# Block transposes of an attention layer: split by head, moved in longer pieces, and one pair of tiles in eight given to TensorE

## Chip, cores and metric

The kernel runs on one core of one Trainium2 chip. The metric is the device time of one execution in microseconds (us). Three runs of the kernel before took 2395.11, 2396.89 and 2406.44 us; the median is 2396.89.

## What is computed

The input x is 4 batches of 1024 tokens by 256 channels, with a context of 77 tokens per batch. Four blocks follow one another: L0 (self attention, cross attention and a feed-forward), L1 (three attention layers of 4 heads), L2 and L3 (cross attention of 16 heads). The change concerns the second and third layers of L1, in which a sequence attends to itself. Cut to one such layer:

```python
def _mha_layer(q, k, v, Wq, bq, Wk, bk, Wv, bv, gamma, beta):   # q = k = v = enc, (4, 1024, 256)
    Q = jax.nn.relu(q @ Wq + bq); K = jax.nn.relu(k @ Wk + bk); V = jax.nn.relu(v @ Wv + bv)
    ...                                                          # 4 heads of 64 channels
    scores = jnp.einsum('hbqd,hbkd->hbqk', Qh, Kh) / jnp.sqrt(jnp.float32(dh))
    scores = jnp.where(key_mask[None, :, None, :] == 0.0, NEG, scores)
    attn = jax.nn.softmax(scores, axis=-1)
    attn = attn * query_mask[None, :, :, None]
    out = jnp.einsum('hbqk,hbkd->hbqd', attn, Vh)
    ...
    return _layer_norm(out + q, gamma, beta)

enc = _mha_layer(...); enc = jax.nn.leaky_relu(enc @ Wff[i] + bff[i], negative_slope=0.2) + enc
```

All of it is float32. The weights of a query (its row of exp(scores)) must be transposed before the product with V, because TensorE contracts over partitions: scores come out with queries on partitions and keys along the row, and the product needs keys on partitions.

## The kernel before

**Items and units.** Work is cut into items: one layer for one batch. The class `Self4` (L1121) is an item of an L1 self layer; there are eight (two layers, four batches), one after the other. An item has 16 units: two pairs of heads p = 0, 1, and for each eight query tiles t of 128 rows (`attend`, L1247). `Pipe.unit` (L139) writes the instructions of one unit in a fixed order of stages: what is due under "full", then the scores of this unit, then what is due under "next", then `pump()`, then "turn", "late" and "col". `Pipe.later(kind, delay, f)` (L132) puts f under a stage of the unit that is `delay` units later. `pump()` adds, spread by given costs, the steps of other items: the end of the item before (statistics, norm L1583 and L1586, the transposes L1396, the feed-forward L1405 to L1412) and the start of the next one (transposes L1167, mask row L1179, values L1190, query and key projections L1226 and L1233).

**Order of instructions.** TensorE (PE) executes in the order in which the program was written. For VectorE (DVE), ScalarE (ACT), GpSimd (POOL) and the SyncE queue (SP) a scheduler decides the order when the program is built; each engine then executes its own list in order, waiting on semaphores.

**One unit.**
- `scores` (L1255): PE computes a 128 x 1024 tile of scores for each of the two heads of the pair, in four products (L1262; the profile shows each as two). They go to two PSUM tiles `ss` of the pool `pb`, which has two buffers; the loop is over key halves outside and heads inside, so the first head's two products are not adjacent.
- For each head, DVE takes the negative maximum along the row (L1273), and ACT takes exp with that bias, summing the row (L1279). The result goes to the tile `PR`, which holds two query tiles and two heads and has two buffers (tag "E"). The exp writes so that 32-wide key blocks of the same residue c of 4 lie together.
- `turned_by_blocks` (L1285), due at "next" of the following unit: DVE transposes every 32 x 32 block of the unit's two heads in place, in one instruction 2048 wide (L1291). After every second tile, 16 DMAs of 128 KB (L1298) move the blocks from 32 partitions of `PR` to 32 partitions of `PT` (two buffers, tag "B"), 8 issued by SP and 8 by POOL in turn. Each moves four pieces of 1 KB from each of 32 partitions.
- `weighted` (L1324), due at "turn" two and three units after that: PE multiplies by V in two halves, 16 matmuls each in the profile (L1334), into a PSUM tile `po`, which ACT copies out (`carry`, L1509, copy L1512).
- `normal` (L1346): PE transposes the result back (L1352), DVE scales it by the row sums (L1357 to L1362) and adds it to x (L1364).

The pool `p1` (L2090) has four PSUM tiles of 128 x 512; projections, transposes and `po` all take theirs from it.

The function `turned` (L1306) is the other way to transpose: 16 PE transposes of 128 x 128 per query tile, four to a PSUM tile, and a copy of each PSUM tile to `PT`. It stands in the kernel for other kinds of mask (`net.blocks` false, L1985 to L1987), and is not executed here. `evac` (L1495) gives copies in turn to DVE and ACT; `carry` gives them to ACT when `net.blocks` is true.

Of the kernel before, what the change touches and what calls it, by code (L numbers as in the profile page):

```python
# [13 lines left out]
ALU = mybir.AluOpType  # L14
AX = mybir.AxisListType
PSUM = bass.MemoryType.PSUM

P = 128
NB, S, C, SC = 4, 1024, 256, 77
NT = S // P  # L20
# [102 lines left out]
class Pipe:  # L123
# [15 lines left out]
    def unit(self, scores=None, cost=0.0):  # L139
        self.call("full")  # L140
        if scores:
            scores()
        self.call("next")
        self.now += cost
        self.pump()
        for kind in ("turn", "late", "col"):
            self.call(kind)
        self.u += 1

    def run(self, items):  # L150
        pump = Pump(self, 1, items[0].start(), [])
        pump.until(lambda: items[0].halves >= 1)
        left = pump.lists[0]
        before = None
        for a, b in zip(items, items[1:]):
            b.prev = a
        for i, item in enumerate(items):
            last = i + 1 == len(items)
            first = left + ([] if last else items[i + 1].start())
            second = (before.end() if before else []) + (item.end() if last else [])  # L160
            left = []
            idle = item.idle()
            self.pump = pump = Pump(self, item.units + idle, item.more() + first, second)
            for _ in range(idle):
                self.unit()
            for scores in item.attend():
                self.unit(scores, item.cost)
            assert last or not any(pump.lists)
            before = item
        while self.due:  # L170
            pump.n = 0
            self.unit()
        pump.n = pump.units - 1
        pump()
# [33 lines left out]
class Cross16(Item):  # L208
# [147 lines left out]
    def scores(self, g, c):  # L356

        net, h = self.net, H16
        nc = net.nc
        e, s = g // 2, g % 2  # L360
        if g % 2 == 0:
            self.pts = net.tile("B", [SC, 2, h.J, 512], name="PT")
        pt = self.pts[:, g % 2]
        pbs = [net.pb.tile([P, 2, 512], F32, tag="pb", name="pb") for _ in range(2)]
        for j in range(h.J):
            rows = slice(32 * j, 32 * j + 32)
            nc.tensor.matmul(  # L367
                pbs[j // 2][:SC, j % 2, :], self.ka[rows, e, 2 * (j % 2) + s, :], self.qt[rows, e, ts(c, 512)],
                start=True, stop=False,
            )  # L370
        for j in range(h.J):
            rows = slice(32 * j, 32 * j + 3 * G)
            nc.tensor.matmul(  # L373
                pbs[j // 2][:SC, j % 2, :], net.pick16[rows, g, :], self.sh[rows, c, :], start=False, stop=True
            )
        for i in range(2):
            nc.scalar.activation(pt[:, 2 * i : 2 * i + 2, :], pbs[i][:SC], AF.Exp, scale=self.l.scale)  # L377
        net.pipe.later("col", 0, lambda: self.weighted(g, c, pt))

    def weighted(self, g, c, pt):  # L380
        net, l, h = self.net, self.l, H16
        nc = net.nc
        po = net.p1.tile([P, 512], F32, tag="p1", name="po")
        for j in range(h.J):
            col = self.head(g, j) * h.vs
            nc.tensor.matmul(  # L386
                po[ts(j, h.slot), :], l.v[:, self.b, col : col + h.vw], pt[:, j, :], start=True, stop=True
            )
        ot = net.tile("OT", [P, 512], name="OT")
        net.evac(ot, po)  # L390
        net.pipe.later("late", 1, lambda: self.normal(g, c, ot))
# [249 lines left out]
class Layer16Self:  # L641


    scale, norm, eps, out, ff, has_wo = 0.25, 1, None, None, None, True
# [168 lines left out]
class LayerFew:  # L813
# [3 lines left out]
    scale, norm, eps, out, ff, has_wo = 0.25, 1, None, None, None, True  # L817
# [303 lines left out]
class Self4(Item):  # L1121
# [133 lines left out]
    def scores(self, p, t):  # L1255
        net = self.net
        nc = net.nc
        ss = [net.pb.tile([P, 2, 512], F32, tag="pb", name="ss") for _ in range(2)]
        for k in range(2):
            for h in range(2):  # L1260
                rows = slice(64 * h, 64 * h + 64)
                nc.tensor.matmul(  # L1262
                    ss[h][:, k, :], self.qk[p][rows, 0, ts(t, P)], self.qk[p][rows, 1, ts(k, 512)],
                    start=True, stop=True,
                )
        if not net.blocks:
            pr = net.tile("E", [P, 2, S], name="PR")
        elif t % 2 == 0:
            self.pr = net.tile("E", [P, 2, 2, S], name="PR")
        for h in range(2):  # L1270
            at = slice(2 * p + h, 2 * p + h + 1)
            s2 = ss[h].rearrange("p k n -> p (k n)")
            nc.vector.tensor_reduce(self.nm[:, t, at], s2, AX.X, ALU.max, negate=True)  # L1273
            if net.blocks:
                out = self.pr[:, t % 2, h, :].rearrange("p (c k i) -> p k c i", c=4, i=32)
                s2 = s2.rearrange("p (k c i) -> p k c i", c=4, i=32)
            else:
                out = pr[:, h, :]
            nc.scalar.activation(out, s2, AF.Exp, bias=self.nm[:, t, at], accum_out=self.sums[:, t, at])  # L1279
        if net.blocks:  # L1280
            net.pipe.later("next", 1, lambda pr=self.pr: self.turned_by_blocks(p, t, pr))
        else:
            net.pipe.later("full", 1, lambda: self.turned(p, t, pr))

    def turned_by_blocks(self, p, t, pr):  # L1285


        net = self.net
        nc = net.nc
        part = pr[:, t % 2].rearrange("p h s -> p (h s)")  # L1290
        nc.vector.transpose(part, part)  # L1291
        if t % 2 == 0:
            return

        pt = net.tile("B", [P, 2, 2, 4, NT, 32], name="PT")
        for c in range(4):
            for a in range(4):
                (nc.sync, nc.gpsimd)[a % 2].dma_start(  # L1298
                    out=pt[ts(c, 32), :, :, a].rearrange("p t h k j -> p (t h) (k j)"),
                    in_=pr[ts(a, 32), :, :, ts(c, 256)].rearrange("p t h n -> p (t h) n"),  # L1300
                )
        state = []
        for half in range(2):
            net.pipe.later("turn", 2 + half, lambda half=half: self.weighted(p, t, pt, half, state))

    def turned(self, p, t, pr):  # L1306

        net = self.net
        nc = net.nc
        if t % 2 == 0:  # L1310
            self.pt = net.tile("B", [P, 2, 2, NT, P], name="PT")
        pts = self.pt
        for h in range(2):
            for k in range(0, NT, 4):
                pm = net.p1.tile([P, 4, P], F32, tag="p1", name="pm")
                for i in range(4):
                    nc.tensor.transpose(pm[:, i, :], pr[:, h, ts(k + i, P)], net.ident)
                net.evac(pts[:, t % 2, h, k : k + 4, :], pm)
        if t % 2:
            state = []  # L1320
            for half in range(2):
                net.pipe.later("col", half, lambda half=half: self.weighted(p, t, pts, half, state))

    def weighted(self, p, t, pts, half, state):  # L1324
        net = self.net
        nc = net.nc
        if half == 0:
            state.append(net.p1.tile([P, 2, P], F32, tag="p1", name="po"))
        po = state[0]
        if net.blocks:  # L1330
            po = po.rearrange("p t (a j) -> p t a j", a=4)
        for k in range(4 * half, 4 * half + 4):
            for h in range(2):
                nc.tensor.matmul(  # L1334
                    po[64 * h : 64 * h + 64], self.v[:, k, 64 * (2 * p + h) : 64 * (2 * p + h) + 64],
                    pts[:, :, h, :, k, :] if net.blocks else pts[:, :, h, k, :], start=k == 0, stop=k == NT - 1,
                )
        if half:
            if t % 4 == 1:
                self.ot = net.tile("OT", [P, 4, P], name="OT")  # L1340
            at = t % 4 - 1
            net.carry(self.ot[:, at : at + 2, :], state[0])
            if at:
                net.pipe.later("late", 1, lambda ot=self.ot: self.normal(p, t - 3, ot))
# [853 lines left out]
```

## Time and profile before

| | |
|---|---|
| median of three runs | 2396.89 us |
| the profiled execution | 2396.79 us |
| its span, first to last instruction | 2394.9 us |
| mean granted TensorE clock | 0.958 |
| busy: PE, DVE, ACT, POOL | 2204.3, 1582.6, 930.2, 380.4 us |
| the eight items of the self layers, from 948.2 to 1872.7 us | 924.5 us |
| busy there: PE, DVE, ACT, POOL | 878.7, 771.2, 440.2, 295.1 us |
| block transposes (L1291) | 128 of 2311 ns |
| block DMAs (L1298) | 1024 of 128 KB |

The profile gives one execution. Busy time of an engine is the union of its instructions' spans; matmuls are pipelined, and a matmul that waits inside its span counts as busy. A group's row gives line, engine, operation, tiles written and read, count, then busy time and mean duration, then the idle time of the engine just before these instructions with what ended it. In a timeline a row is start, duration, engine, line, operation, with neighbours of one kind merged; in brackets stands idle time before it and what ended it. SPq marks the issuing of DMAs by SP.

### The profile page before, as it was taken

Reading aid. Unit: us, or ns where it says so; the run is one execution under the profiler, and the core shown is the slowest. Engines: PE = TensorE matmul, PEld = TensorE weight load, DVE = VectorE, ACT = ScalarE, POOL = GpSimd, SP = SyncE. Lnnn points to the kernel's source line nnn. Section 1 sums busy time; section 2 is a strip of 40 time slices with the busy share of each in tenths; the row PEclk is TensorE's granted clock in tenths of the full one; section 3 lists DMA queues with packets and bytes.
Section 4 is the critical chain, followed back from the end, with each engine's and each line's share of the span. In section 5 each row is a group of like instructions: output and inputs, shape, how many; then the busy total and the mean of one; then the engine's idle time right before and its main releaser. Section 6 shows DMA issues by size and latency. Waiting matters only on the chain. (4 is left out here: it accounts for less than half of the span.)

```text
span 2394.9 us, 31195 instructions
## 1 busy us (share of the span) xinstructions
PE 2204.3 (92%) x11035; PEld 1204.8 (50%) x11035; DVE 1582.6 (66%) x3167; ACT 930.2 (39%) x1828; POOL 380.4 (16%) x648
## 2 busy tenths in 40 slices
PE   6899999999898979999999899999999899999996
PEld 3565446566577655545454445454545344444442
DVE  6665553534424565888888788888888656656765
ACT  2222332222232355545454454444444234434333
POOL 2000000000000000333333233333333100000000
PEclk8999989989998998999999999999999899999988
DMA  5000010000000000667776577766787400000000
GB/s 147 1 3 14 5 36 1 1 3 5 12 1 7 1 5 1 146 147 152 151 156 144 123 151 157 151 142 141 148 163 143 97 5 1 5 1 1 27 18 28
DMA packets 148677, 158.01 MB, mean 66 GB/s; under 512 B 51432, under 2 KB 130849, under 8 KB 148513
## 3 DMA queue, kind: packets, MB, share of 16 engines
q1 hardware_dynamic: 122161, 85.63, 17.2%
q0 software_dynamic: 25296, 69.24, 13.1%
q8 instruction: 91, 1.49, 0.3%
q10 hardware_dynamic: 1056, 1.05, 0.1%
q14 instruction: 73, 0.60, 0.1%
HBM read 17.41 MB, written 4.19 MB: 9 GB/s over the span
## 5 line engine op out<-in xcount | busy, mean ns | idle before, releaser
L1279 ACT ACTIVATE PR<-ss,nm 128x1024 f32<-128x1024 f32 x256 | 284.7, 1114 | 366.2 <-DVE nm L1273 290.2
L1291 DVE STREAM_TRANSPOSE PR<-PR 128x2048 f32<-128x2048 f32 x128 | 295.8, 2311 | 128.9 <-ACT PR L1279 114.3
L1298 POOL DMA_DIRECT2D PT<-PR x512 | 279.6, 554 | 577.7 <-PE ss L1262 236.7
L1262 PE MATMUL ss<-QK 64*128 64x512 f32 x1024 | 324.8, 628 | 28.8 <-ACT PR L1279 28.5
L1273 DVE TENSOR_REDUCE nm<-ss 128x1 f32<-128x1024 f32 x256 | 299.6, 1210 | 13.8 <-PE ss L1262 13.8
L377 ACT ACTIVATE PT<-pb 77x1024 f32<-77x1024 f32 x192 | 185.4, 1015 | 193.2 <-PE pb L373 193.2
L1334 PE MATMUL po<-PT,V 128*64 128x256 f32 x2048 | 251.1, 387 | 5.1 <-DMA PT<-PR 5.1
L281 DVE TENSOR_REDUCE mx<-pa 128x4 f32<-128x308 f32 x384 | 161.4, 470 | 83.7 <-PE pa L276 82.5
L1262 PEld LDWEIGHTS ss<-QK 64*128 64x128 f32 x1024 | 113.3, 187 | 176.8 <-ACT PR L1279 99.7
L1334 PEld LDWEIGHTS po<-PT,V 128*64 128x64 f32 x2048 | 136.6, 137 | 108.4 <-issue 51.1
L276 PE MATMUL pa<-KA,QT 64*128 64x308 f32 x768 | 169.1, 486 | 14.0 <-DVE mx L281 12.8
L1545 POOL TENSOR_TENSOR pw<-va,minus_half 128x4 f32<-128x4 f32 (+1 forms) x28 | 38.8, 1384 | 714.5 <-DVE va L1543 542.0
L386 PE MATMUL po<-PT,Vc 77*32 77x512 f32 x768 | 140.4, 639 | 7.6 <-ACT PT L377 7.0
L276 PEld LDWEIGHTS pa<-KA,QT 64*128 64x128 f32 x768 | 84.3, 193 | 99.1 <-issue 37.0
L604 PE MATMUL pp<-hF,w 128*128 128x256 f32 x512 | 116.9, 382 | 0.0
L367 PE MATMUL pb<-QT,KA 32*77 32x512 f32 x768 | 114.1, 665 | 0.0
L619 PE MATMUL pp<-w,hid 128*128 128x256 f32 x512 | 113.7, 379 | 0.0
L619 PEld LDWEIGHTS pp<-w,hid 128*128 128x128 f32 x512 | 97.0, 190 | 16.5 <-issue 2.2
L604 PEld LDWEIGHTS pp<-hF,w 128*128 128x128 f32 x512 | 95.6, 190 | 18.2 <-issue 6.0
L266 PE MATMUL pp<-hT,wq 128*128 128x512 f32 x192 | 98.0, 646 | 5.5 <-ACT hT L1507 5.0
L1536 DVE BATCH_NORM_STATS2 st<-x 128x6 f32<-128x256 f32 x256 | 97.7, 403 | 3.2 <-DMA x<-in_x 2.3
L1405 PE MATMUL pp<-wo,hE 128*128 128x256 f32 x384 | 96.4, 393 | 1.6 <-ACT hE L1512 1.6
(256 smaller groups left out, 3079.5 us busy)
## 6 DMA issues: line engine op xcount, KB each, us to landing
PT<-PR SPq DMA_DIRECT2D x512, 128.0 KB
PT<-PR POOLq DMA_DIRECT2D x512, 128.0 KB, 4.9
x<-in_x SPq DMA_DIRECT2D x4, 1024.0 KB
out<-x SPq DMA_DIRECT2D x8, 512.0 KB
w<-in_ff_w SPq DMA_DIRECT2D x2, 1024.0 KB
gb<-in_norms POOLq DMA_DIRECT2D x5, 256.0 KB, 6.6
wk<-in_l_wk SPq DMA_DIRECT2D x10, 128.0 KB
wv<-in_l_wv SPq DMA_DIRECT2D x5, 256.0 KB
```

Of the source, the lines that this page charges most:

```text
L276: nc.tensor.matmul(pas[i], self.qt[rows, e, ts(t, P)], self.ka[rows, e, :, :], start=True, stop=True)
L281: nc.vector.tensor_reduce(out, pas[i].rearrange("p (j s) k -> p j s k", s=2), AX.X, ALU.max, negate=True)
L377: nc.scalar.activation(pt[:, 2 * i : 2 * i + 2, :], pbs[i][:SC], AF.Exp, scale=self.l.scale)
L386: nc.tensor.matmul(po[ts(j, h.slot), :], l.v[:, self.b, col : col + h.vw], pt[:, j, :], start=True, stop=True)
L604: nc.tensor.matmul(pp[:, i, :], self.w1[:, cc, ts(f + i, P)], s["hT"][:, cc, ts(q, 2 * P)], start=cc == 0, stop=cc == NC - 1)
L619: nc.tensor.matmul(pp[:, u, :], s["a"][:, f, ts(u, P)], self.w2[:, f, :], start=f == 0, stop=f == NF - 1)
L1262: nc.tensor.matmul(ss[h][:, k, :], self.qk[p][rows, 0, ts(t, P)], self.qk[p][rows, 1, ts(k, 512)], start=True, stop=True,)
L1273: nc.vector.tensor_reduce(self.nm[:, t, at], s2, AX.X, ALU.max, negate=True)
L1279: nc.scalar.activation(out, s2, AF.Exp, bias=self.nm[:, t, at], accum_out=self.sums[:, t, at])
L1291: nc.vector.transpose(part, part)
L1298: (nc.sync, nc.gpsimd)[a % 2].dma_start(out=pt[ts(c, 32), :, :, a].rearrange("p t h k j -> p (t h) (k j)"), in_=pr[ts(a, 32), :, :, ts(c, ...
L1334: nc.tensor.matmul(po[64 * h : 64 * h + 64], self.v[:, k, 64 * (2 * p + h) : 64 * (2 * p + h) + 64], pts[:, :, h, :, k, :] if net.blocks e ...
```

## The change

Three things, all in `scores`, `turned_by_blocks`, `turned` and `weighted`:

1. `PR` and `PT` are laid out anew. `PR` is now [4 key residues c, 2 tiles, 2 heads, 256] per partition, and `PT` is [4 source blocks a, 2 tiles, 2 heads, 8, 32]. Each of the 16 DMAs then moves one piece of 4 KB from each of 32 partitions. SP issues 12 of them (a = 0, 1, 2) and POOL 4 (a = 3).
2. The block transposes are one instruction per head, 1024 wide, and are written in `scores` right after the exps; `issue_after` keeps them behind the second reduction in DVE's list.
3. For p = 1 and tiles 2 and 3, the fourth of the item's eight DMA groups is replaced by `turned`: 32 PE transposes and 8 copies by ACT. Tile 2 is due at "next" two units later, tile 3 at "turn" one unit later, both in the unit of tile 4; the products with V are due in the units of tiles 6 and 7, where they were before.

```diff
+        blocks = net.blocks and (p, t // 2) != (1, 1)
         if not net.blocks:
             pr = net.tile("E", [P, 2, S], name="PR")
         elif t % 2 == 0:
-            self.pr = net.tile("E", [P, 2, 2, S], name="PR")
+            self.pr = net.tile("E", [P, 4, 2, 2, S // 4], name="PR")
+        if net.blocks and not blocks:
+            pr = self.pr.rearrange("p c t h n -> p (c t h n)")[:, ts(t % 2, 2 * S)].rearrange("p (h n) -> p h n", h=2)
...
-            nc.vector.tensor_reduce(self.nm[:, t, at], s2, AX.X, ALU.max, negate=True)
-            if net.blocks:
-                out = self.pr[:, t % 2, h, :].rearrange("p (c k i) -> p k c i", c=4, i=32)
+            reduced = nc.vector.tensor_reduce(self.nm[:, t, at], s2, AX.X, ALU.max, negate=True)
+            if blocks:
+                out = self.pr[:, :, t % 2, h, :].rearrange("p c (k i) -> p k c i", i=32)
...
-        if net.blocks:
-            net.pipe.later("next", 1, lambda pr=self.pr: self.turned_by_blocks(p, t, pr))
+        if net.blocks and not blocks:
+            net.pipe.later(("next", "turn")[t % 2], 2 - t % 2, lambda: self.turned(p, t, pr))
+        elif net.blocks:
+            with net.tc.issue_after(reduced.ins):
+                for h in range(2):
+                    part = self.pr[:, :, t % 2, h, :]
+                    nc.vector.transpose(part, part)
+            if t % 2:
+                net.pipe.later("next", 1, lambda pr=self.pr: self.turned_by_blocks(p, t, pr))
...
-        part = pr[:, t % 2].rearrange("p h s -> p (h s)")
-        nc.vector.transpose(part, part)
-        if t % 2 == 0:
-            return
-        pt = net.tile("B", [P, 2, 2, 4, NT, 32], name="PT")
+        pt = net.tile("B", [P, 4, 2, 2, NT, 32], name="PT")
         for c in range(4):
             for a in range(4):
-                (nc.sync, nc.gpsimd)[a % 2].dma_start(
-                    out=pt[ts(c, 32), :, :, a].rearrange("p t h k j -> p (t h) (k j)"),
-                    in_=pr[ts(a, 32), :, :, ts(c, 256)].rearrange("p t h n -> p (t h) n"),
+                (nc.gpsimd if a == 3 else nc.sync).dma_start(
+                    out=pt[ts(c, 32), a].rearrange("p t h k j -> p (t h k j)"),
+                    in_=pr[ts(a, 32), c].rearrange("p t h n -> p (t h n)"),
                 )
...
-                net.evac(pts[:, t % 2, h, k : k + 4, :], pm)
+                net.carry(pts[:, t % 2, h, k : k + 4, :], pm)
...
-                net.pipe.later("col", half, lambda half=half: self.weighted(p, t, pts, half, state))
+                when = ("turn", 2 + half) if net.blocks else ("col", half)
+                net.pipe.later(*when, lambda half=half: self.weighted(p, t, pts, half, state, False))
```

More of the change, by code (lines that the diff above doesn't have):

```diff
@@ L1321, in turned, with weighted @@
             for half in range(2):
-                net.pipe.later("col", half, lambda half=half: self.weighted(p, t, pts, half, state))
-    def weighted(self, p, t, pts, half, state):
+                when = ("turn", 2 + half) if net.blocks else ("col", half)
+                net.pipe.later(*when, lambda half=half: self.weighted(p, t, pts, half, state, False))
+    def weighted(self, p, t, pts, half, state, blocks=True):
         net = self.net
@@ L1329, in weighted @@
         po = state[0]
-        if net.blocks:
+        if blocks:
             po = po.rearrange("p t (a j) -> p t a j", a=4)
@@ L1335, in weighted @@
                     po[64 * h : 64 * h + 64], self.v[:, k, 64 * (2 * p + h) : 64 * (2 * p + h) + 64],
-                    pts[:, :, h, :, k, :] if net.blocks else pts[:, :, h, k, :], start=k == 0, stop=k == NT - 1,
+                    pts[:, :, :, h, k, :].rearrange("p a t j -> p t a j") if blocks else pts[:, :, h, k, :], start=k == 0, stop=k == NT - 1,
                 )
```

## Prediction

> **What bounds the kernel now.** I read the page first. In its forty slices the change can touch only the 17th to 32nd, where DMA is busy at 4 to 8 tenths: the two self layers of L1, eight items (two layers by four batches) of 16 units each. A unit is one query tile of one pair of heads. Then I asked for engine times in the eight windows from one item's first scores to the next one's; two of them, and the sum of the eight:
>
> ```profile
> 1413.40:1526.40 113.00, 108.32 (x545) 54.11 (x543) 96.28 (x123) 55.59 (x119) 37.57 (x67) 1.00 0.73 154
> 1643.60:1758.00 114.40, 109.70 (x546) 54.51 (x544) 96.42 (x122) 53.33 (x105) 37.01 (x66) 1.00 0.71 150
> sum 924.50, PE 878.73 PEld 433.56 DVE 771.23 ACT 440.16 POOL 295.10; mean PE 109.84 PEld 54.20 DVE 96.40 ACT 55.02 POOL 36.89
> ```
>
> After the length come the busy times of PE, PEld, DVE, ACT and POOL, the clock and the DMA share. PE is busy 878.7 of 924.5 us, idle 45.8; DVE 771.2. PE looks like the bound, but the groups and the timeline say how much of its busy time is waiting:
>
> ```profile
> L1262 PE MATMUL ss<-QK 64*128 64x512 f32 x1024 | 324.8, 628 | 28.8 <-ACT PR L1279 28.5
> L1291 DVE STREAM_TRANSPOSE PR<-PR 128x2048 f32<-128x2048 f32 x128 | 295.8, 2311 | 128.9 <-ACT PR L1279 114.3
> ```
> ```profile
> 1558.51 1.99 PE L1262 MATMUL ss<-QK 64*128 64x512 f32 x8
> ```
> ```profile
> 1314.50 1.95 PE L1334 MATMUL po<-PT,V 128*64 128x256 f32 x16
> 1314.81 2.31 DVE L1273 TENSOR_REDUCE nm<-ss 128x1 f32<-128x1024 f32 x2
> ...
> 1316.03 1.11 ACT L1279 ACTIVATE PR<-ss,nm 128x1024 f32<-128x1024 f32 x1 [2.91 <-DVE nm L1273]
> ...
> 1317.16 1.11 ACT L1279 ACTIVATE PR<-ss,nm 128x1024 f32<-128x1024 f32 x1
> ...
> 1317.28 3.11 PE L1262 MATMUL ss<-QK 64*128 64x512 f32 x8 [0.83 <-ACT PR L1279]
> ...
> 1318.39 2.31 DVE L1291 STREAM_TRANSPOSE PR<-PR 128x2048 f32<-128x2048 f32 x1 [1.27 <-ACT PR L1279]
> ...
> 1320.63 2.32 DVE L1273 TENSOR_REDUCE nm<-ss 128x1 f32<-128x1024 f32 x2
> ```
>
> A unit's eight score matmuls take 1.99 us when both PSUM tiles are free (the row at 1558.51), and 3.11 where the first head's tile is free and the second head's exp is still reading its own (1317.28 against an exp that ends at 1318.27). The matmul group sums to 324.8 us; 128 units at 1.99 are 254.7. So 70.1 us of PE's "busy" is this stretch, and with the 45.8 idle PE loses **116 us** in the stage. The cause is in the last lines: DVE reduces both heads, then sits idle 1.27 us until both exps are done, transposes 2048 wide until 1320.70, and is late for reductions that could start at 1320.63. It has no slack, so any other DVE work (norms, residuals) delays the next exps and, through them, PE. That idle is 114.3 us in the group's row.
>
> **The change, part by part.**
>
> *Transposes split by head.* Each 2048-wide transpose becomes two of 1024, the first waiting for the first head's exp alone. In the unit above it could start at 1317.15 (reductions end at 1317.12, first exp at 1317.14), and the second follows as the second exp (1318.27) is done. A half costs at least 2.311/2 = 1.16 us, at most the 1.21 of a 1024-wide reduction plus the 0.18 by which 2.311 exceeds 2048 elements at two back-to-back reductions' 2.31 per 2048 (nothing), so 1.16 to 1.39; I take 1.2. End: 1317.15 + 2.4 = 1319.55 against 1320.70, **1.15 us of slack per unit**. In the built program the halves stand directly behind their unit's reductions nearly everywhere, as the whole ones did; only norm work stands between in three or four units of an item.
> [...]
>
> *What this is worth to PE.* I walked item 1413.4 to 1526.4. Its losses by unit, from the timeline: stretches and idle of 1.3 us in unit 2, 3.4 in unit 3, 0.6 and 1.1 in units 6 and 7, 2.0 in unit 11, 1.6 in unit 12, 1.1 in unit 15, 0.1 elsewhere: 11.2. With 1.15 us of slack, units 6, 7 and 15 lose nothing. In units 2 and 3 norm work of some 2.7 us lies between halves and next reductions (seven L1583 and L1586 at 0.47, statistics besides), so about 2 of 4.7 remain; 1.7 of that was PE waiting for a PSUM tile behind an exp (L1167), and the built order on ACT now copies one such tile before the exps. Units 11 and 12 are bound by the loop of scores, reduction and exp itself: PE there has 1.99 + 0.5 + 1.95 = 4.45 us of work and the second exp ends at 1.99 + 0.23 + 2.32 + 1.2 = 5.75, so about 2.5 of 3.6 remain. That leaves 4.8, and 6.4 are recovered. Five items are like this: 32 us. The other three (the windows of 110.5, 124.5 and 114.7) lose 12.5, 20.3 and 20.5 by the same count; 6.9 of the second is a wait for the thirds DMA that stays. I take half of the remaining 46.4: 23. **Recovered: 55**, bounds 0 and 116 - 6.9 = 109.
>
> *One pair of tiles in eight by TensorE.* For p = 1, tiles 2 and 3: two tiles by two heads by eight blocks, 32 transposes an item, in eight PSUM tiles copied by ACT. The nearest row is L1167 at 1552.78: 12 in 1.53 us, 0.127 each; 16 run in 1.99 elsewhere. So 4.0 us an item, **32 us** of PE that nothing hides, since PE is the bound. Eight copies at 0.58 (L1512, 128x512) are 4.7 us of ACT in one unit; ACT is busy 55.6 of 113, so it has room overall. But in the built order the first four and a key projection stand ahead of that unit's exps, which then end some 9.9 us after the unit's start. PE has 1.99 + 2 + 0.5 + 2.4 + 1.95 + 2 + 0.66 = 11.5 us in that unit, so it should hide; if PSUM (four tiles, one held by po) binds, 0.5 to 2 us an item, up to 16. DVE loses two 2.31 transposes an item, 37 us in all, which gives it slack in units where it is not late.
> [...]
>
> *Block DMAs.* 56 pairs of tiles instead of 64, each still 16 DMAs of 128 KB, in contiguous 4 KB runs on both sides instead of 1 KB. SP now issues 12 and POOL 4; it was 8 and 8.
>
> ```profile
> L1298 SPq DMA_DIRECT2D PT<-PR x512: 585/806/1982, 965.3 to 1894.0; - x171
> ```
>
> SP needs 8.0 us for its eight: the first at 0.59, later ones 1.0 to 1.5, held back by transfers under way. The last packet ends 11.4 to 13.4 us after the transpose; a pair of units takes 11.7 to 16. Twelve issues are 7.1 us at 0.59 and 11.9 at the present mean of 0.99, still under 14.3, the mean pair (924.5/64). Whether 4 KB runs move faster no row shows for SBUF to SBUF; by the trace's packets (medians) loads with 4 KB rows took 159 ns each, POOL's 4 KB packets here 311 and SP's 1 KB ones 81. So a pair lands between half the time and the same time. I take no loss and no gain: PE waited 5.1 us in all for PT, and the weighted products come two units later. Also on SP, the mask row (L1179) and thirds (L2061) queue behind 12 issues instead of 8: 4 x 0.8 = 3 us, against units of lead; once the thirds had none, 3 us either way.
> [...]
>
> *Layout of PR and PT.* Exps write runs of 32 in both; the products read runs of 32 in both. Rows 1.11 and 1.95 us kept; nothing.
>
> **Sum.** 32 - 55 = -23. The profiled execution took 2396.8 us (span 2394.9), the median shown is 2396.9: **2374**.
>
> **Rivals.**
> 1. *PE's added work outweighs.* If the norm work and the loop, not the late transposes, hold most stretches, only the losses at the turned pair (units 11 and 12, some 1.5 us an item, 12 in all) go: +32 - 12 = +20, 2417. For it: DVE is not the busiest engine. Against: 114.3 us of DVE's idle ends on ACT's exps. It decides from less than 32 us recovered.
> 2. *SP becomes the bound.* Above 14.3/12 = 1.19 us per issue the queue falls behind, and exps wait for PR (two buffers). At 1.3: (15.6 - 14.3) x 56 = +73, less 23: 2447. Against: eight issues ran at 0.99 with half the bytes on POOL.
> 3. *A draw.* 32 to 35 recovered: 2394.
> 4. *DVE runs clear.* Norm bursts are absorbed too, and losses fall to 25 us: 32 - 91 = -59: 2338.
> That the change does nothing of what it says is excluded: the built program has the halves of 14 units and the 32 PE transposes in each item, in the places told above.
>
> **Chances.** Forecast 0.45 (own range 2358 to 2388), rival 1 0.16, 2 0.05, 3 0.17, 4 0.17. Faster by over 0.5% (below 2385; about what a measurement of this kernel can tell): 0.59. Within 0.5%: 0.22. Slower: 0.19. The range leaves out rival 2 and the far ends of 1 and 4: 2330 to 2420. The outer bounds of the sum are 32 - 109 and 32 + 16.
>
> **What would show it.** Right: L1262's matmuls near 2.2 us a unit (280 us busy), DVE's idle before the transposes below 40 us, PE transposes at 32 us in two groups of 16, item windows near 110. Wrong: halves well over 1.2 us; PE waiting for ACT's copies in the turned unit; ACT waiting for DMA in many units; SP issues over 1.19 us; or longer stretches at half clock (0.5 in the clock row) as PE gets denser.

## The result, and the profile after

The changed kernel takes 2412.83 us (median of 20 runs, 2403.23 to 2420.3), the kernel before 2401.68 us on the same chip (20 runs): a ratio of **1.005, 95% interval 1.0034 to 1.0066**. It is slower by about 11 us, where 2374 had been forecast. The profiled execution has a span of 2404.5 us against 2394.9, at the same clock (0.959 against 0.958).

The page's groups of the changed kernel, which answer to the two shown of before (after the bar: busy us, mean ns, then the engine's idle time ahead of them and what ended it):

```profile
L1262 PE MATMUL ss<-QK 64*128 64x512 f32 x1024 | 318.6, 626 | 13.4 <-ACT PR L1282 12.3
L1289 DVE STREAM_TRANSPOSE PR<-PR 128x1024 f32<-128x1024 f32 x224 | 267.7, 1226 | 81.6 <-ACT PR L1282 68.3
```

The halves take 1.23 us, as priced. But the score matmuls' stretch, forecast to fall to 280 us, only fell from 324.8 to 318.6, and VectorE's idle time behind the exps fell from 114.3 to 68.3 us, not below 40. So VectorE has its slack, and the exps still come late. The waits, for the stage alone (from 948 us on before, from 953 us on after), say what ScalarE did instead (engine, what it wrote, its line, whom it waited for, us in total, times, longest). Before:

```profile
ACT V L1194 <- PE pv L1190: 9.7, 3, 6.9
ACT QK L1233 <- PE pp L1231: 5.3, 3, 3.7
```

After:

```profile
ACT V L1194 <- PE pv L1190: 51.9, 15, 6.1
ACT QK L1233 <- PE pp L1226: 34.2, 15, 3.5
ACT QK L1233 <- PE pp L1231: 31.6, 12, 3.6
ACT low L1417 <- PE pp L1412: 27.0, 11, 3.8
```

ScalarE waits for projections of the next item (values L1190, keys and queries L1226 and L1231) and of the previous one (output L1412), to copy them out of PSUM. That idle time would cost nothing if nothing stood behind it. The timeline of the changed kernel shows what does:

```profile
1454.30 2.35 DVE L1276 TENSOR_REDUCE nm<-ss 128x1 f32<-128x1024 f32 x2 [0.51 <-PE ss L1262]
...
1454.84 1.99 PE L1190 MATMUL pv<-wv,hT 128*128 128x256 f32 x8
...
1456.88 0.84 ACT L1194 ACTIVATE V<-pv,f 128x256 f32<-128x256 f32 x2 [4.00 <-PE pv L1190]
...
1457.60 1.11 ACT L1282 ACTIVATE PR<-ss,nm 128x1024 f32<-128x1024 f32 x1
...
1458.84 2.37 DVE L1289 STREAM_TRANSPOSE PR<-PR 128x1024 f32<-128x1024 f32 x2 [1.74 <-ACT PR L1282]
```

The first head's maximum is ready at about 1455.5 (half of two reductions that end at 1456.65). Its exp starts at 1457.60: ScalarE's list has the value eviction ahead of it, and that waits until 1456.83 for its matmuls. The exp is 2.1 us late, VectorE idles 1.74 us, and the slack that the split made is gone. I counted this over all 128 units: the time from the end of the first head's reduction to the start of its exp, less 0.1 us. It sums to 5.6 us before and to **104.2 us after**, 103.4 of it in 45 units that are more than 0.2 us late; there the instruction just ahead is the key/query eviction (L1233) for 45.4 us, the value eviction (L1194) for 27.2 and the output eviction (L1417) for 22.2. In the other direction the split did its work: the time from a unit's last score matmul to its first reduction, less 0.24 us, fell from 95.3 to 38.4 us in all.

No line of the diff touches these evictions. They are written as before, and so are the exps; what differs is the order in which the build lists the instructions. In ScalarE's order one of the three evictions stands ahead of an exp that the program writes before it 8 times before, 53 times after (two value evictions in a row count as one), and once in the changed kernel with the block DMAs issued 8/8 as before. So:

- **Theory A**: issuing twelve of sixteen block DMAs on SP costs the time, by moving ScalarE's list: evictions that must wait stand ahead of exps.
- **Theory B**: the 12/4 issuing costs time on the queues themselves; the order is a bystander.
- **Theory C**: the pair on TensorE costs more than was recovered, as rival 1 had it.

The expectations of numbers 1 to 4 use the letters the other way round: there B is the pair, and in numbers 1 and 2 C is the queues. From number 5 on B is the queues, as here.

### The profile page after: what moved, and what is told of

Same layout as the page of the kernel before. It is cut to its first block, busy times and chain, and to the rows that moved or that the text cites. A ratio compares the mean times of both kernels' runs of the same rounds, so it can differ in the third digit from the quotient of the medians.

```text
span 2404.5 us, 31100 instructions
## 1 busy us (share of the span) xinstructions
PE 2227.9 (93%) x11291; PEld 1228.9 (51%) x11291; DVE 1564.8 (65%) x3263; ACT 962.4 (40%) x1892; POOL 210.0 (9%) x360
## 5 line engine op out<-in xcount | busy, mean ns | idle before, releaser
L1262 PE MATMUL ss<-QK 64*128 64x512 f32 x1024 | 318.6, 626 | 13.4 <-ACT PR L1282 12.3
L1289 DVE STREAM_TRANSPOSE PR<-PR 128x1024 f32<-128x1024 f32 x224 | 267.7, 1226 | 81.6 <-ACT PR L1282 68.3
L1304 POOL DMA_DIRECT2D PT<-PR x224 | 109.3, 494 | 799.4 <-PE ss L1262 178.4
L1412 PE MATMUL pp<-wo,hE 128*128 128x256 f32 x384 | 96.4, 393 | 1.4 <-ACT hE L1519 1.4
```

The source lines that it names most:

```text
L1262: nc.tensor.matmul(ss[h][:, k, :], self.qk[p][rows, 0, ts(t, P)], self.qk[p][rows, 1, ts(k, 512)], start=True, stop=True,)
```

## Experiments

All ratios are to the kernel before on the same chip. "Stage" is the trace's time from the first score matmul of these layers to the last, "exps late" the count above. Before: stage 924.5 us, of it PE idle 45.8. Stage, idle time and lateness come from one execution of each kernel; its stretches at half clock alone differ (23.9 us of the stage in number 1, 20.5 in number 5), so two or three us decide nothing.

| kernel | ratio, 95% interval | stage us | PE idle | exps late |
|---|---|---|---|---|
| the change (12/4) | 1.005 (1.0034 to 1.0066) | 937.7 | 31.9 | 104.2 |
| 1: the change with 8/8 | 0.9907 (0.987 to 0.9944) | 907.3 | 30.9 | 1.5 |
| 2: the change, all other ScalarE work held behind exps | 1.0307 (1.0271 to 1.0344) | 1007.2 | 100.8 | 4.4 |
| 3: split alone (8/8) | 0.9702 (0.9669 to 0.9734) | 863.6 | 21.8 | 1.8 |
| 4: pair alone (8/8) | 1.0056 (1.0029 to 1.0084) | 945.7 | 45.3 | 1.4 |
| 5: the change, three evictions held behind exps | 0.9913 (0.9885 to 0.9941) | 909.1 | 30.5 | 31.7 |
| 6: split and 4 KB layout, 8/8 | 0.9717 (0.9685 to 0.9748) | 863.4 | 22.9 | 0.5 |
| 7: split and pair, 8/8 | 0.9893 (0.9859 to 0.9928) | 906.9 | 32.6 | 1.6 |
| 8: 12/4 alone | 1.0206 (1.0171 to 1.0241) | 980.7 | 59.5 | 99.5 |
| 9: as 7, the pair's copies shared | 0.987 (0.985 to 0.9891) | 897.7 | 29.7 | 0.4 |
| 10: split, 12/4 | 1.0065 (1.0045 to 1.0084) | 938.3 | 42.2 | 110.7 |
| 11: as 10, three evictions held behind exps | 0.9802 (0.9767 to 0.9836) | 879.8 | 33.9 | 17.2 |
| 12: split and 4 KB layout, 12/4 | 1.0033 (1.0007 to 1.0059) | 938.2 | 42.1 | 110.6 |

**1. The change with the issuing put back.**

```diff
-                (nc.gpsimd if a == 3 else nc.sync).dma_start(
+                (nc.sync, nc.gpsimd)[a % 2].dma_start(
```

> The changed kernel, with one thing undone: SP and POOL issue 8 and 8 of the 16 block DMAs again instead of 12 and 4 (the pieces stay 4 KB). Theory A (the order in ScalarE's list): the share of 12 made the scheduler put projections' copies ahead of exps, which start 104 us too late in all; with 8 and 8 the built list has only one such key or query projection ahead of an exp, so lateness falls below 15 us and the time to about 2375, 1% below the kernel before. Theory B (rival: the TensorE transposes cost more than the stalls that go): the time stays at or above 2400. Theory C (SP's twelve issues themselves are slow, the transfers late): the time falls too, but exps were late because of transfers, so the profile after should have shown ScalarE waiting for DMAs, and forcing ScalarE's order while keeping 12 and 4 should not help.

Measured 0.9907: this one line is worth 1.4% (1.005 - 0.9907), 30 us of the stage. The exps start on time. At the place shown above, its timeline has the value eviction behind both exps, and the transposes follow at once:

```profile
1433.10 2.35 DVE L1276 TENSOR_REDUCE nm<-ss 128x1 f32<-128x1024 f32 x2
...
1434.40 1.11 ACT L1282 ACTIVATE PR<-ss,nm 128x1024 f32<-128x1024 f32 x1 [2.87 <-DVE nm L1276]
...
1435.64 2.37 DVE L1289 STREAM_TRANSPOSE PR<-PR 128x1024 f32<-128x1024 f32 x2
...
1436.60 0.83 ACT L1194 ACTIVATE V<-pv,f 128x256 f32<-128x256 f32 x2
```

It says where the time is, not yet whether the order or the queues cost it, since both changed. The order changed on VectorE too: between the change and number 1 at least 117 of the stage's 967 instructions on ScalarE and 237 of 1076 on VectorE stand elsewhere (the fewest that must be moved to turn one trace's order into the other's). Theory C falls here: with the pair kept, the kernel is 0.9% faster than before.

**2. The order forced, 12/4 kept.** Everything that ScalarE does for other work in a unit is put behind that unit's second exp.

```diff
-        self.call("next")
...
+        with self.tc.issue_after(self.exp.ins) if self.exp else ExitStack():
+            self.call("next")
+            self.now += cost
+            self.pump()
...
-            nc.scalar.activation(out, s2, AF.Exp, bias=self.nm[:, t, at], accum_out=self.sums[:, t, at])
+            net.pipe.exp = nc.scalar.activation(out, s2, AF.Exp, bias=self.nm[:, t, at], accum_out=self.sums[:, t, at])
```

> The changed kernel with its 12 and 4 issues, and what is traced after a unit's scores held behind that unit's second exp in ScalarE's list. Theory A: lateness of the exps falls from 104 us to below 15, and the time to about 2375 to 2385, as with 8 and 8 issues; the forced order costs a little where a copy could have gone into ScalarE's idle time. Theory B: 2400 or more. Theory C: no better than the changed kernel, 2410.

Measured 1.0307, where theory A had 2375 to 2385 us: inconclusive, since the edit held back too much. The exps were on time (4.4 us late), but PE's idle time rose to 100.8 us, most of it in units 3 and 4 of an item, 4.2 us each on average. Its granted clock was at half speed for 119.5 us of the stage, against 30.7 in the change. In those units the next item's start hung on work now late (PE's waits, stage alone; lines are numbered two higher here):

```profile
PE pm L1176 <- DVE neg L1159: 42.5, 7, 9.4
PE pt L1169 <- ACT hT L1521: 27.0, 6, 5.0
```

**3 and 4. One part alone, on the kernel before.** Number 3 has only the two halves, with `PR`, `PT`, the DMAs and the pair as before:

```diff
-        part = pr[:, t % 2].rearrange("p h s -> p (h s)")
-        nc.vector.transpose(part, part)
...
+            with net.tc.issue_after(reduced.ins):
+                for h in range(2):
+                    part = self.pr[:, t % 2, h, :]
+                    nc.vector.transpose(part, part)
```

> The kernel before with only the transposes split by head: old layout, 1 KB pieces, 8 and 8 issues, all pairs by DMA. The reductions that DVE starts late (95 us in all before, 38 after the change) should fall to about 40. Theory A: without TensorE's added 32 us, about 2397 - 50 = 2350. Theory B: about 2380 (the stalls that go are few). A worth of nothing, 2397, would refute the slack that the prediction gave to the split.

Measured 0.9702, the fastest of all; the stage loses 60.9 us. Its page:

```profile
L1289 DVE STREAM_TRANSPOSE PR<-PR 128x1024 f32<-128x1024 f32 x256 | 307.6, 1229 | 23.2 <-ACT PR L1282 14.5
L1262 PE MATMUL ss<-QK 64*128 64x512 f32 x1024 | 290.6, 619 | 8.8 <-ACT PR L1282 8.5
```

VectorE's idle time behind the exps falls from 114.3 to 14.5 us and the stretch to 290.6: the picture that the prediction drew for the whole change. Beside the halving, the place in VectorE's list moved a little: the transposes stand directly behind their unit's reductions in 98 of 128 units here and in 72 before, and ahead of the next unit's reductions in all of both. What this is worth by itself wasn't tested.

Number 4 has only the pair (`blocks = net.blocks and (p, t // 2) != (1, 1)`, `turned` for that pair, `carry` in it).

> The kernel before with only the one pair of tiles in eight transposed by TensorE: whole transposes, old layout, 1 KB pieces, 8 and 8. It adds 32 us to TensorE and takes two late transposes an item away. Theory A and the prediction: +32 less some 12 in stalls at the turned pair, 2417. Theory B: the full 32 or more, 2430.

Measured 1.0056. Alone, the pair costs about 13 us (0.56% of 2406); the stage grew by 21.2.

**5. Only the three evictions held, 12/4 kept.** The cut of number 2 that does not hold back the rest:

```diff
+                with net.pipe.behind():
                     nc.scalar.activation(self.v[:, t + i, :], pv[:, i, :], AF.Relu, scale=self.f[:, t + i : t + i + 1])
...
+        with net.pipe.behind():
             nc.scalar.activation(out, pp, AF.Relu, bias=l.bias[:, i, p : p + 1], scale=(0.125, 1.0)[i])
...
+            with net.pipe.behind():
                 nc.scalar.mul(low, pp, 0.2)
```

Here `behind()` is `issue_after` for the unit's last exp written so far. The DMAs, the pair and the layout are those of the change.

> The changed kernel whole, 12/4 issuing kept, with one thing forced: the ScalarE evictions of key/query projections, value projections and the scaled output projection (L1233, L1194, L1417) stand behind the second exp of their unit in ScalarE's list. Theory A (the 12/4 split costs time only through the order of ScalarE's list): 0.985 to 0.995 of the kernel before, like the version with 8/8 issuing (0.9907), and exps that start late behind their maximum fall from 104 us to under 25. Theory B (the queues themselves carry 12/4 worse): 1.00 to 1.01, with the exps on time.

Measured 0.9913 against 0.9907 with 8/8. ScalarE's waits for the projections are nearly gone (in the change 51.9 us for values, 34.2 and 31.6 for keys and queries, 27.0 for the output; a few lines are numbered higher here):

```profile
ACT low L1425 <- PE pp L1419: 2.6, 2, 1.5
ACT QK L1240 <- PE pp L1237: 2.0, 2, 1.4
ACT V L1200 <- PE pv L1195: 0.7, 1, 0.7
```

This tells A from B: with the twelve issues left on SP, the order alone gives back 28.6 of the 30.4 us. The traces' orders say how alone: against the change, SP's and POOL's are the same, 8 of VectorE's 1076 instructions moved and 72 of ScalarE's 967. VectorE still differs from number 1 by 232, so its own new order isn't what cost the time either. The exps are 31.7 us late, over the 25 expected, now mostly behind the copies that `carry` makes, of transposes and of the products with V (26.2 in all), which I had not held.

**6 and 7. What the rest of the change costs beside the split.** Number 6 is the change with 8/8 and `blocks = net.blocks` (no pair); number 7 is number 1 with the 1 KB layout of before.

> Transposes split by head and the 4 KB layout, 8/8 issuing, no pair on TensorE. If the 21 us a stage that the version with 8/8 loses against the split alone are the pair's work on TensorE: 0.968 to 0.973, as the split alone (0.9702). If they are the layout's: 0.985 to 0.992.

> Transposes split by head and the pair on TensorE, 1 KB pieces as before, 8/8 issuing. If the pair costs what it adds once VectorE has slack: 0.985 to 0.992. If the layout is what costs: 0.972 to 0.978 (the split alone and the 0.6% that the pair alone cost).

Measured 0.9717 and 0.9893. The layout is worth nothing (stage 863.4 against 863.6, with every engine's instructions in the same order in both), and the pair costs 1.9% beside the split (0.9893 - 0.9702), 43.3 us of the stage. (The "21 us" in the first expectation was too small: numbers 1 and 3 differ by 43.7 in the stage.) PE's busy time grows by 32.5 us (841.8 to 874.3) and its idle time by 10.8 (21.8 to 32.6). Both lie in the unit of the transposes, which takes 13.49 us instead of 8.25 (means over six items) and idles 1.62 instead of 0.38. Its timeline in number 7:

```profile
1252.15 1.97 PE L1323 MATMUL pm<-ident,PR 128*128 128x128 f32 x16
1252.68 1.11 ACT L1282 ACTIVATE PR<-ss,nm 128x1024 f32<-128x1024 f32 x1 [2.12 <-DVE nm L1276]
...
1253.78 0.58 ACT L1519 COPY PT<-pm 128x512 f32<-128x512 f32 x1
...
1254.25 1.13 ACT L1282 ACTIVATE PR<-ss,nm 128x1024 f32<-128x1024 f32 x1
...
1255.35 1.57 ACT L1519 COPY PT<-pm 128x512 f32<-128x512 f32 x3
...
1255.99 1.98 PE L1226 MATMUL pp<-hT,wk 128*128 128x512 f32 x4 [0.93 <-ACT PT L1519]
```

Sixteen transposes fill the four PSUM tiles by 1254.12; the copies alternate with exps, and PE waits 0.93 us for a tile.

**8. The issuing alone.** The kernel before with only the opposite of the edit of number 1.

> The kernel before with nothing changed but twelve of sixteen block DMAs issued by SP and four by POOL (1 KB pieces, whole transposes). Its ScalarE list puts key/query, value and output evictions ahead of exps of an earlier unit 80 times, against 7 before. Theory A (order of ScalarE's list): 1.01 to 1.04. Theory B (the queues): SP then issues 12 x 0.99 = 11.9 us in a pair's 14.3 us, so no loss from issuing alone: 1.00 to 1.005 unless transfers come late.

Measured 1.0206, exps 99.5 us late: as theory A says, in a kernel without any other part of the change.

**9. The pair's copies shared between VectorE and ScalarE** (`carry` back to `evac` in `turned`).

> Split by head and the pair on TensorE with 1 KB pieces and 8/8 issuing (0.9893 with all eight copies of the pair on ScalarE), its copies now in turn on VectorE and ScalarE. If the 1.2 us an item that TensorE loses at unit 12 beyond its transposes is the wait for ScalarE's copies behind the exps: idle there from 1.62 to about 0.6 us, 0.985 to 0.988. If VectorE has no room there: 0.989 to 0.992.

Measured 0.987: the unit's idle time falls from 1.62 to 0.84 us, the unit from 13.49 to 12.55. The wait was there as read; by the times alone, whose intervals overlap, numbers 7 and 9 can't be told apart. The pair still costs 34.1 us (897.7 - 863.6).

**10 to 12. 12/4 with the split.** Number 10 is number 3 with 12/4, number 11 is number 10 with the three evictions held, number 12 is number 10 with the 4 KB layout.

> Split by head alone with 1 KB pieces (0.9702 with 8/8), now with 12/4 issuing. ScalarE's list puts key/query, value and output evictions ahead of an earlier unit's exps 66 times, against 1 with 8/8. If the order is what costs: 0.984 to 0.992, exps more than 80 us late in all. If what 12/4 costs needs the pair or the 4 KB layout beside it: under 0.975.

> Split by head alone, 1 KB pieces, 12/4 issuing (1.0065), with the key/query, value and output evictions held behind the exps of their unit in ScalarE's list. If the order is all that 12/4 costs: 0.968 to 0.976, as with 8/8 (0.9702). If 12/4 with 1 KB pieces also brings blocks late: 0.98 to 1.00, with waits of VectorE or TensorE on these transfers.

> Split by head and the 4 KB layout with 12/4 issuing, no pair on TensorE: ScalarE's list stands as in the version with 1 KB pieces (66 evictions ahead of earlier exps). If the order sets the time whatever the piece: 1.003 to 1.009, as that one (1.0065). If 4 KB pieces take off what SP's longer issuing costs: 0.985 to 1.000.

Measured 1.0065, 0.9802 and 1.0033. 12/4 costs the split 74.7 us of the stage, more than I expected, and turns the fastest kernel into one slower than before. Holding three evictions gives back 58.5 of them. By the order alone nearly all should have come back; 16.2 us stay, and 0.9802 lies at the edge that late blocks were to give. But the waits on block transfers are no longer than in number 3 (TensorE 5.4 us against 5.9, mostly just behind the stage; exps 21.3 against 57.9; VectorE 0.9). On average over six items 2.4 us of them an item lie in unit 3 (9.38 us against 6.99), where PE's waits for the copies of transposes of x sum to 14.0 us against 4.7 in number 3: the same kind of work, other copies. That these would go if they too were placed well wasn't tried. Number 11 also differs from number 3 in VectorE's order (250 of 1108), so the 16.2 us stay open.

Part of what 12/4 costs here may come through TensorE's clock: in the stage it was granted at half speed for 17.1 us in number 3, 44.4 in number 10 and 27.3 in number 11. Counting half of such time as lost, I estimate up to 13.7 of the 74.7 us (half of 44.4 - 17.1), and 5.1 of the 16.2. What brought the half speed on wasn't tested.

The piece makes no difference here either (938.2 against 938.3, the instructions again in one order), though the expectation had left room for it.

## Why the prediction was wrong

**Transposes split by head: right.** Each half was put at 1.2 us and took 1.23. The recovery was put at 55 us of the 116; the split alone gives back 60.9. Unit by unit the walk held nearly as well: in the five items like the walked one, number 3 loses 4.5 to 5.5 us where 4.8 were put. Of that 0.3 lie in unit 2 and 1.6 in unit 3, 1.9 in all where 2 were put; units 11 and 12 keep 1.7 where 2.5 were put, but units 6 and 7 keep 0.4 and 0.6 where nothing was to stay. The upper bound of 1.39 for a half had no ground: the 0.18 in it stands in no row.

**The claim on L1167 was read from one item's list.** It said that the built order copies the waiting PSUM tile before the exps. In the changed kernel unit 3 idles 2.08 us on average against 2.04 before, and this wait (L1167 behind a copy of hT) sums to 11.3 us against 8.6 before. With 8/8 it is 4.7.

**The pair on TensorE: right in its main term.** 32 us of PE were put in, and PE's busy time grew by 32.5 in number 7, 0.127 us a transpose. The further wait for PSUM was bounded at up to 16 us and taken as hidden. PE's idle time grows by 10.8 with 8/8 (number 7), so there it doesn't hide: the pair costs 43.9 us and not 32. In the change itself unit 12 takes 11.58 us and idles 0.09, as the walk of 11.5 us said, since there four copies and a key eviction do stand ahead of the exps.

**Block DMAs: this is the step that failed.** "I take no loss and no gain" priced the queues, and in the change it held for them. Twelve issues for two tiles take 8.3 us at the measured mean of 0.69 in the changed kernel (0.95 before by the same count), far under 14.3 (924.5/64 is in fact 14.4), so rival 2 is out, and in number 5 12/4 costs 1.8 us once the order is mended. The reading that SP's later issues take 1.0 to 1.5 us was rough: by place in the eight they average 0.60, 0.64, 0.71, 1.10, 1.12, 1.37, 1.34 and 0.72, and of twelve in number 8 only the fourth and fifth are over 1 us. An issue that starts with no packet of SP's and POOL's queues under way took 0.62 us on average in the kernel before and 0.56 in the change, with eight or more under way 1.10 and 0.73. Longer issues and transfers under way go together there; that the one causes the other no run here shows. What wasn't priced is that the choice of the issuing engine goes into the build's ordering of all engines. I looked at where the halves and the pair's transposes stood in the built lists, and at ScalarE's list around one unit, not at where the exps stood against evictions that wait for PE. The 12/4 issuing, put at nothing, cost **30.4 us** in the change, and 28.6 of them came by that order.

The sum with measured terms, added in the order split, layout, pair, 12/4, is 2396.8 - 60.9 - 0.2 + 43.9 + 30.4 = 2410.0 (the 43.9 is the stage of number 1 less that of number 6), against a median of 2412.83. Of the 36 us by which it stands above the forecast, 30.4 come from the step put at nothing, 11.9 from the pair beyond its 32, and the split gives 5.9 more than put.

These terms are not independent. With 8/8 the pair costs 43.9 us, with 12/4 nothing (937.7 against 938.2): in that order it relieves units 14 and 15 by 2.9 us an item (7.29 and 7.81 us in number 12, 6.03 and 6.17 in the change) and units 1 to 4 and 13 by 3.2, against 3.7 more in unit 12 and 1.6 in others, and one of the three evictions stands ahead of earlier exps 53 times instead of 66. So the sum above is one order of adding the parts, and by another 12/4 costs 75 us and the pair none.

**Rivals.** Rival 1's 2417 came near the time, but not by its mechanism: it decides below 32 us recovered, and the split recovers 60.9. None of the rivals named a changed order of work that the diff does not touch. Why the build lists the evictions earlier when SP has twelve issues was not settled; that it does so, and what it costs, is.

ScalarE kept to the order of its list: a value eviction that waits until 1456.83 holds up an exp whose maximum was ready at 1455.5, until 1457.60. The queues themselves carry 12/4 at a cost of 1.8 us as far as number 5 goes; the 16.2 us of number 11 stay open.

**The version to keep** is number 3, the split alone: 0.9702 (0.9669 to 0.9734), 3.5% faster than the change.

## What to carry to other kernels

Where a build decides the order, an edit that looks free on its own engine can move instructions on others: compare every engine's list, above all for instructions that wait for another engine and now stand ahead of those on the critical loop. Add the time from "operand ready" to "start" for the loop's instructions over all units; that one count (5.6 against 104.2 us) names the fault faster than busy shares do. Measure the parts of a bundled change one by one: here one part was worth -3.0%, and the others took it all back.

## What the runs showed of the hardware

- A half transpose costs more than half: 1.229 us in number 3 against 2.311/2 = 1.156 before, so 0.15 us a pair of halves. Two in a row overlap a little (2.37 us in the timeline), so 128 more instructions added only 11.8 us of VectorE's busy time in number 3 (307.6 - 295.8), 0.09 each, and the stage is still 60.9 us shorter there.
- From SBUF to SBUF, 4 KB pieces moved no faster than 1 KB ones: in numbers 6 and 3 SP's packets took 313 ns (median in the stage) with 4 KB against 81 with 1 KB, about four times as long, and the stage is equal to 0.2 us; POOL's packets are of 4 KB in both. What 4 KB shortens is issuing: at 8/8 SP's issues of 128 KB average 0.88 us against 0.95 (numbers 6 and 3).
